# Attention scores from split queries and keys in three passes, with queries turned by one product and a transfer that exchanges halves

## The chip, the cores and the metric

The kernel runs on one core of a Trainium2 chip. A core has a TensorE (PE, the matmul array; PEld is its weight load), a VectorE (DVE), a ScalarE (ACT), a GpSimd (POOL) and a SyncE (SP), which here only issues DMA transfers. Each engine works off its own instructions in program order; semaphores tie the engines together. SBUF is the on-chip memory, PSUM the memory that the PE writes. The metric is the device time of one execution in microseconds; lower is better. The median of three runs before the change is 781.5 us (781.18 to 782.31).

## The reference

One transformer layer in fp32: cross-attention with 32 query heads and 8 key/value heads of 128, then a gated feed-forward part whose weights go through a 16-level block quantization. There are 8 batches of 128 rows, 512 wide.

```python
x = x + attention(layernorm(x), ctx, ctx, mask, Wq, Wk, Wv, Wo)
x = x + ffn(layernorm(x), w1, w2, w3)

# attention
q = apply_rope((query @ Wq).reshape(b, t, h, d))
k = apply_rope((key @ Wk).reshape(b, t, kv_h, d))
v = (value @ Wv).reshape(b, t, kv_h, d)
logits = jnp.einsum('btkgd,bTkd->bkgtT', q, k) * ATTN_MULT
logits = 30 * jnp.tanh(logits / 30)
weights = softmax(jnp.where(mask, logits, -1e30))
attn = jnp.einsum('bkgtT,bTkd->btkgd', weights, v)
return attn.reshape(b, t, h * d) @ Wo

# apply_rope; rotate_half(x) is (-x2, x1) for the halves x1, x2 of the last axis
x * cos(phase) + rotate_half(x) * sin(phase)

# ffn; dq1 to dq3 are w1 to w3 after nf4_quant_dequant: each block of 64 is divided
# by its largest magnitude, set to the nearest of 16 levels, and multiplied back
h = silu(x @ dq1.T) * (x @ dq2.T)
return h @ dq3.T
```

## The kernel before

**Products.** A number is kept as two fp32r parts, `hi` and `lo` (`split`, L154: ACT casts to `hi`, then POOL or DVE subtracts to get `lo`). A product of split operands takes three passes, hi·lo, hi·hi and lo·hi (`product`, L165), all added up in one PSUM bank. The scores are the exception: one fp32 matmul (L719, `pl`), which the profile shows as two instructions. So are the product with the values (L732, `pv`) and the transposes (L162).

**Stages.** First come the projections of keys and values (`k_proj`, `v_proj`), whose results go to DRAM (`kr_d`, `v_d`), and the first four query heads. They are one list of tiles (L611). In the tile loop (L668) a tile's evacuation is emitted one tile later, and what follows it one more. Then comes the attention loop (L807): 64 rounds. A unit `u` is one key/value head and one half of the batches; each of its four rounds takes one batch with four query heads. Round `i` holds, in the PE's order: `q_proj` of one head for unit `u + 1` (`pq`), `project(i-3)` (`po`), `turn(i-2)` (`pt_a`), `values(i-1)` (`pv`) and `scores(i)` (`pl`). The last rounds have no `q_proj`. The feed-forward part follows (`pg`, `pu`, then `pd`).

**Turning a head.** `rope` (L453) has ACT copy the two halves of 64 partitions crosswise (L461, L462), DVE multiply by the cosine (L463), POOL multiply the exchanged copy by the signed sine (L464) and add (L465) into `qr[u]`, a fresh tile for each unit, two buffers in turn.

**Scores.** ACT takes tanh and exp (L722, L723), POOL multiplies by the mask (L725). `values` divides by the sum (`ad`), `turn` transposes and splits (`aT`), and `project` adds the result to `acc`.

**The quantizer.** Its steps are spread over the stages by `pump(n)`, which adds `n` to a credit and emits steps until it is used up. A step is a comparison on ACT (L194, `nm_w`) and one on DVE (L200, or L198 for the first, `nc_w`); there are 15 for a unit of 1024 columns, and a last product (L278 or L236). The next unit is loaded midway (`w_w`, `s_w`) and normalized on POOL (L204). Its finished tiles are split and sent to DRAM (`store`, L284, transfer at L287).

**Order.** Buffers are few (raw weights three, `wq` six, `vt` two), and a load is issued by SP in program order once its buffer is free. PSUM is eight banks: two `q` banks, which `pq` and `pt_a` share in turn, one `s` for scores, one `wo`, two for `pv`, two for the quantizer (`c`).

Of the kernel before, what the change touches and what calls it, by code (L numbers as in the profile page):

```python
# [62 lines left out]
def block_kernel(ctx: ExitStack, tc: tile.TileContext, x, ctxt, mask, wq, wk, wv, wo, w1, w2, w3, w12t, w3_t,  # L63
# [145 lines left out]
    class Down(Unit):  # L209
# [30 lines left out]
        def store(self, h):  # L240
            pool, tag, bufs = (f1, "w3t", 8) if h < 8 else (nf, "nf_t", 2) if h < 10 else (xp, "wide", 2)
            t = w3t[h] = pool.tile([P, 2, KT, P], F32R, tag=tag, name=f"w3t_{h}", bufs=bufs)
            own = t.rearrange("p i k c -> p i (k c)")[:self.p].rearrange("p i (c e) -> p i e c", e=4)
            split(own[:, 0], own[:, 1], self.part(self.w, h).rearrange("p (e c) -> p e c", e=4), Q)

    class Up(Unit):
# [20 lines left out]
        def load(self):  # L267
            self.w = self.tile("nf_w", "w")
            n = min(H - self.start, self.r)
            if n < self.r:  # L270
                Q.memset(self.w, 0.0)
            for j, part in self.parts(self.w):
                nc.sync.dma_start(part[:, :, :n],
                                  w12t[j].rearrange("k p h -> p k h")[:, :, self.start:self.start + n])
            self.s = self.scale(1)

        def finish(self):
            V.tensor_tensor(self.w, self.c, self.s, ALU.mult)  # L278
            for j, part in self.parts(self.w):
                for i in range(self.r // P):  # L280
                    fresh.append(lambda tag, h=self.start // P + i, j=j, src=part[:, :, i * P:(i + 1) * P]:
                                 self.store(h, j, src))

        def store(self, h, j, src):  # L284
            t = nf.tile([P, 2, KT, P], F32R, tag="nf_t", name=f"dqt_{h}_{j}")
            split(t[:, 0], t[:, 1], src, Q)
            nc.sync.dma_start(w12t_d[h, j], t.bitcast(F32))  # L287

    class Scales:
# [5 lines left out]
        def load(self):  # L295
            self.w = nf.tile([P, 2 * D], F32, tag="nf_t", name=f"ws_{self.h}")
            rows = slice(self.h * P, min(H, self.h * P + P))
            n = rows.stop - rows.start
            if n < P:
                Q.memset(self.w, 0.0)  # L300
# [22 lines left out]
    class Scales3:  # L323
# [8 lines left out]
        def load(self):  # L332
            self.w = nf.tile([P, 2 * D], F32, tag="nf_t", name=f"ws3_{self.u}")[:, :self.cols.stop - self.cols.start]
# [12 lines left out]
        def turn(self, tag):  # L346
# [4 lines left out]
            def later():  # L351
                art = nf.tile([self.nb, 2, P], F32, tag="nf_t", name="art3")
# [11 lines left out]
    fresh, to_store, stored = [], [], []  # L364
# [8 lines left out]

    def quantize():
        invert = None
        for i, u in enumerate(units):
            for k, b in enumerate(NEG[::-1] + POS):
                u.bound(b)
# [3 lines left out]
                for when, s in found.get(i, ()):  # L382
                    if k == when - 4:
# [6 lines left out]
                if i + 1 < len(units):  # L390
                    if k == (6 if isinstance(units[i + 1], Down) else 10):
                        units[i + 1].load()
                    if k == 13:
                        units[i + 1].normalize()
# [23 lines left out]

    def wide(name, pool=xp):
# [5 lines left out]
    with ExitStack() as c1:  # L425

        xT = [wide(f"xT_{i}") for i in range(2)]
        cosq = a1.tile([P, T], F32, name="cosq")
        sgnq = a1.tile([P, T], F32, name="sgnq")
        mt = a1.tile([P, T], F32, name="mt")  # L430
        qr = {}
# [15 lines left out]
        def columns(w, h, name):  # L447
# [3 lines left out]
            return t, lambda: split(t[:, 0], t[:, 1], raw, V if name == "wk_3" else Q)  # L451

        def rope(dst, src, cos, sgn, name, engine=None, apart=False):  # L453
# [4 lines left out]

            c = src4 if engine is V and apart else tp.tile([P, 4, T], F32, tag="t1", name=f"rc_{name}")
            s = tp.tile([P, 4, T], F32, tag="t2", name=f"rs_{name}")  # L460
            S.copy(s[:hd], src4[hd:])  # L461
            S.copy(s[hd:], src4[:hd])  # L462
            V.tensor_tensor(c, src4, every(cos), ALU.mult)  # L463
            Q.tensor_tensor(s, s, every(sgn), ALU.mult)  # L464
            return lambda: (engine or Q).tensor_tensor(dst, c, s, ALU.add)  # L465
# [5 lines left out]

        def q_proj(u, g):
            kv, half = divmod(u, 2)
            if g == 0:
                qr[u] = a1.tile([P, 4, G, T], F32, tag="qr", name=f"qr_{u}", bufs=2)
            pq = bank("q", f"pq_{u}_{g}")
            w, t = wqt[kv, g], xT[half]
            product(pq, [((w[:, 0, k], w[:, 1, k]), (t[:, 0, k], t[:, 1, k])) for k in range(KT)])
            return lambda: rope(qr[u][:, :, g, :], pq, cosq, sgnq, f"q{u}_{g}", V if u < 2 else None, u == 1)


        with ExitStack() as c3:
# [6 lines left out]
            vs = a1.tile([P, 4, 4, HD], F32, tag="qr", name="vs", bufs=2)  # L489
# [55 lines left out]
            def k_proj(kv, half):  # L545
# [11 lines left out]
                def later():  # L557
                    kr = kv1.tile([P, 512], F32, tag="kr", name=f"kr_{kv}_{half}")
                    add = rope(kr.rearrange("p (b t) -> p b t", t=T), pk, tab[:, 0], tab[:, 1], f"k{kv}_{half}",
# [8 lines left out]
            def v_proj(j, b):  # L568
# [5 lines left out]
                def later():  # L574
                    v = vs[:, b % 4]
# [7 lines left out]
            def masks():  # L583
# [12 lines left out]
                def count():  # L596
# [3 lines left out]
                    V.tensor_tensor(cosq, tab[:, 0], some, ALU.mult)  # L600
                    V.tensor_tensor(sgnq, tab[:, 1], some, ALU.mult)
# [4 lines left out]
            def normal(b):  # L606
# [8 lines left out]
                     ("v", 1, 1), ("k", 7, 1)] + [("v", 1, b) for b in range(2, B)] + [("q", 0, g) for g in range(G)]  # L615
            make = {"k": k_proj, "v": v_proj, "q": q_proj}
# [40 lines left out]
            for b in range(B):  # L657
                plan[10 + (b + 1) // 2].append(lambda b=b: ln.sums(b))
                plan[18 + 2 * b].append(lambda b=b: xn.update({b: ln.rows(b)}))
                plan[19 + 2 * b].append(lambda b=b: turned.update({b: normal(b)}))  # L660
                plan[20 + 2 * b].append(lambda b=b: turned[b]())
# [5 lines left out]
            evac, last = None, None  # L667
            for n, (what, i, j) in enumerate(tiles):  # L668
                if n == 4:

                    last()
                    last = None
                done = evac() if evac else None
# [8 lines left out]
                if 9 <= n < 19:  # L682
                    store()
                if n >= 33:
                    store("wo")
                if n >= 15 and n != 17:
                    pump(2 if n in (24, 28) else 1)
            last()
            evac()()
# [8 lines left out]
        def load_o(kv, g):  # L698
# [3 lines left out]
            todo["o", kv, g] = lambda: split(t[:, 0], t[:, 1], raw, Q if kv or g > 1 else V)  # L702

        def load_kv(kv):
            for half in range(2):
                krt[kv, half] = at.tile([P, 512], F32, tag="kr", name=f"krt_{kv}_{half}", bufs=4)
                nc.sync.dma_start(krt[kv, half], kr_d[kv, half])
# [8 lines left out]
        def scores(i):  # L716
            u, kv, b, bb = where(i)
            pl = bank("s", f"pl_{i}")
            E.matmul(pl, krt[kv, u % 2][:, bb * T:(bb + 1) * T], qr[u][:, bb].rearrange("p g t -> p (g t)"),  # L719
                     start=True, stop=True)  # L720
# [26 lines left out]

        load_kv(0)
        early.append(tp.tile([P, 512], F32, tag="xn", name="raw_wo_0"))
        for g in range(G):  # L750
            load_o(0, g)
        end_store()
# [22 lines left out]
        def gate_up(half, h, pool=None, between=None):  # L775
# [18 lines left out]
            def later():  # L794
                sg = tp.tile([P, 512], F32, tag="t1", name=f"sg_{half}_{h}")
# [3 lines left out]

        due = {1: [("o", 0, g) for g in range(G)]}  # L800
# [6 lines left out]
        for i in range(N):  # L807
            u, kv, b, bb = where(i)
            s8 = i % 8
            if kv + 1 < NKV:  # L810
                if s8 == 0:
                    load_kv(kv + 1)
                if s8 < 4:
                    load_q(kv + 1, s8)
                else:
                    load_o(kv + 1, s8 - 4)
                due.setdefault(i + (2 if i < 4 else 1), []).append(("q" if s8 < 4 else "o", kv + 1, s8 % 4))
            tiles = {0: (0, 1), 1: (2,), 2: (3,), 3: ()}.get(i, (bb,)) if u + 1 < 2 * NKV else ()
            later = [q_proj(u + 1, g) for g in tiles]
            if i != 2:  # L820
                later = [f() for f in later[:1]] + later[1:]
            if i == 0:
                later.pop(0)()
            if i == 1:
                todo[due[1].pop(0)]()
            if i > 3:
                store()
                end_store()
            pump(1.5 if 3 < i < 58 else 1 if i == 58 else 0.5 if i == 3 else 0)
# [4 lines left out]
            if 0 <= i - 2:  # L834
                turn(i - 2)
            if 59 <= i < 63:
                ln.sums(i - 59)
            if i == 1:

                later.pop(0)()  # L840
            if 0 <= i - 1:
                values(i - 1)
            if i == 1:
                todo[due[1].pop(0)]()
            scores(i)
# [138 lines left out]
```

## Time and profile before

| what | value |
|---|---|
| median of the runs | 781.5 us |
| the profiled execution, whole | 781.61 us |
| its span | 779.8 us |
| instructions | 11217 |
| granted PE clock | 1.00 |
| bytes moved by DMA | 102.44 MB, mean 131 GB/s |
| PE busy, 200 to 250 us | 50.00 of 50 us |
| DVE busy, 200 to 250 us | 41.14 us |
| ACT busy, 200 to 250 us | 41.72 us |
| POOL busy, 200 to 250 us | 39.12 us |

The span is the time from the first to the last instruction on the chip; the execution's own time has a little around it. A group's line in the profile gives line, engine, operation, what it writes and reads, how often, then its busy time, the mean duration in ns, and the idle time of its engine just before it with what ended that idle time.

### The profile page before, as it was taken

To read this page: it belongs to the slowest core of one execution; us is meant where nothing else is said; L and a number is where in the kernel's file an instruction comes from. 1 tells how busy PE (TensorE), PEld (TensorE's weight loads), DVE (VectorE), ACT (ScalarE), POOL (GpSimd) and SP (SyncE) were. 2 spreads that over 40 slices of the span, in tenths; PEclk is the share of its full clock that TensorE was granted. 3 is DMA by queue.
4 is the path that set the end of the run, shared out by engine and by line. 5 is a ranking of instruction groups with operands and counts; after the bars stand their busy time and mean duration, and the time that the engine had idled before them with its cause. 6 is when DMAs were issued, how large, how long until landed. Compare 5 with 4: busy or idle time off the path is not lost.

```text
span 779.8 us, 11217 instructions
## 1 busy us (share of the span) xinstructions
PE 774.1 (99%) x3736; PEld 627.2 (80%) x3736; DVE 624.6 (80%) x850; ACT 586.2 (75%) x830; POOL 462.3 (59%) x404
## 2 busy tenths in 40 slices
PE   9999999999999999999999999999999999999998
PEld 7787877888878787877878787888778888888887
DVE  6758876988887887888888878888778697899971
ACT  7448768988897978788787879898742686789740
POOL 2559636887878778877788787878650222332100
PEclk9999999999999999999999999999999999999999
DMA  6967743546254615536245523413150235633011
GB/s 217 307 190 213 226 148 116 177 121 176 56 172 140 195 49 160 149 92 214 64 146 160 156 71 103 139 53 127 57 215 1 67 98 160 188 114 107 1 54 55
DMA packets 74497, 102.44 MB, mean 131 GB/s; under 512 B 7848, under 2 KB 44392, under 8 KB 74440
## 3 DMA queue, kind: packets, MB, share of 16 engines
q1 hardware_dynamic: 72136, 93.34, 39.5%
q0 software_dynamic: 2304, 8.39, 3.6%
q8 instruction: 30, 0.49, 0.3%
q14 instruction: 27, 0.22, 0.1%
HBM read 79.32 MB, written 22.38 MB: 130 GB/s over the span
## 4 chain that ended last, share of the span: by engine, by line
PE 94%; DMA 2%; ACT 2%; DVE 1%; issue 1%; POOL 0%; SPq 0%; POOLq 0%; DVEq 0%; ACTq 0%
PE pq L170 23%; PE po L170 23%; PE pd L170 8%; PE pg L170 8%; PE pu L170 8%; PE pv L732 7%; PE pl L719 7%; PE pt_a L162 4%; PE pvp L170 4%; PE pk L170 1%; PE pk L541 1%; DMA s_w<-scale_d 1%; DMA scale_d<-art 1%; DMA kr_d<-kr 1%; PE pt_y L162 0%
## 5 line engine op out<-in xcount | busy, mean ns | idle before, releaser
L200 DVE SCALAR_TENSOR_TENSOR nc_w<-nm_w,nc_w 128x1024 f32<-128x1024 bf16 (+1 forms) x238 | 284.5, 1195 | 54.6 <-ACT nm_w L194 43.4
L194 ACT ACTIVATE nm_w<-w_w,bias 128x1024 bf16<-128x1024 f32 (+1 forms) x255 | 275.7, 1115 | 26.9 <-POOL w_w L204 18.3
L170 PE MATMUL pq<-xT,wq 128*128 128x512 f32 x768 | 208.7, 421 | 0.0
L170 PEld LDWEIGHTS pq<-xT,wq 128*128 128x128 f32 x768 | 143.7, 188 | 56.1 <-issue 23.3
L170 PE MATMUL po<-wo,aT 128*128 128x512 f32 x768 | 188.8, 395 | 0.0
L170 PEld LDWEIGHTS po<-wo,aT 128*128 128x128 f32 x768 | 143.2, 188 | 33.4 <-issue 2.4
L725 POOL TENSOR_TENSOR th<-th,mt 128x512 f32<-128x512 f32 x64 | 83.7, 1308 | 86.3 <-ACT th L723 76.3
L464 POOL TENSOR_TENSOR rs_q<-rs_q,sgnq 128x512 f32<-128x512 f32 x64 | 82.6, 1290 | 13.6 <-ACT rs_q L462 13.4
L722 ACT ACTIVATE th<-pl 128x512 f32<-128x512 f32 x64 | 38.3, 598 | 50.9 <-PE pl L719 49.6
L465 POOL TENSOR_TENSOR qr<-rc_q,rs_q 128x512 f32<-128x512 f32 x56 | 72.6, 1297 | 0.0
L732 PE MATMUL pv<-vt,th 128*128 128x129 f32 x512 | 67.8, 275 | 0.0
L719 PE MATMUL pl<-qr,krt 128*128 128x512 f32 x128 | 65.6, 594 | 0.0
L170 PE MATMUL pg<-xT,w 128*128 128x512 f32 x264 | 63.7, 390 | 0.0
L170 PE MATMUL pu<-xT,w 128*128 128x512 f32 x264 | 63.5, 389 | 0.0
L732 PEld LDWEIGHTS pv<-vt,th 128*128 128x128 f32 x512 | 62.2, 192 | 0.4 <-POOL th L725 0.4
L170 PE MATMUL pd<-w3t,hs 128*128 128x512 f32 (+3 forms) x297 | 60.6, 366 | 0.0
L204 POOL TENSOR_TENSOR w_w<-w_w,s_w 128x1024 f32<-128x1024 f32 (+1 forms) x17 | 40.0, 2352 | 34.2 <-DMA s_w<-scale_d 32.0
L170 PEld LDWEIGHTS pd<-w3t,hs 128*128 128x128 f32 (+1 forms) x297 | 51.4, 189 | 9.2
L170 PEld LDWEIGHTS pu<-xT,w 128*128 128x128 f32 x264 | 49.5, 188 | 10.3
L170 PEld LDWEIGHTS pg<-xT,w 128*128 128x128 f32 x264 | 49.3, 188 | 10.1
L156 POOL TENSOR_TENSOR w3t<-w_w,w3t 128x512 fp32r<-128x512 f32 (+1 forms) x11 | 17.2, 1566 | 65.5 <-ACT w3t L155 65.5
L155 ACT CAST aT<-pt_a 128x512 fp32r<-128x512 f32 x64 | 36.6, 571 | 25.2 <-PE pt_a L162 25.2
(119 smaller groups left out, 1097.3 us busy)
## 6 DMA issues: line engine op xcount, KB each, us to landing
w12t_d<-dqt SPq DMA_DIRECT2D x22, 512.0 KB
s_w<-scale_d SPq DMA_DIRECT2D x40, 256.0 KB
raw_wq<-in_L_xattn_Wq SPq DMA_DIRECT2D x32, 256.0 KB
raw_wo<-in_L_xattn_Wo SPq DMA_DIRECT2D x32, 256.0 KB
w<-w12t_d POOLq DMA_DIRECT2D x16, 512.0 KB, 4.5
s_w<-scale_d SPq DMA_DIRECT2D x86, 64.0 KB
ws<-in_L_ffn_w SPq DMA_DIRECT2D x20, 256.0 KB
w_w<-in_w12t SPq DMA_DIRECT2D x10, 512.0 KB
```

The costliest lines, as they stand in the source:

```text
L155: S.copy(hi, src)
L162: E.transpose(pt[:, k * P:(k + 1) * P], src[:, k * P:(k + 1) * P], ident)
L170: E.matmul(out, a, b, start=start and i + j == 0, stop=stop and i == n - 1 and j == 2)
L194: S.activation(m, self.w, AF.Relu, bias=bias[:self.p, i:i + 1], scale=BIG if up else -BIG)
L200: V.scalar_tensor_tensor(self.c, m, step, self.c, ALU.min, ALU.subtract if i == POS[0] else ALU.add)
L204: Q.tensor_tensor(self.w, self.w, self.s, ALU.mult)
L464: Q.tensor_tensor(s, s, every(sgn), ALU.mult)
L465: return lambda: (engine or Q).tensor_tensor(dst, c, s, ALU.add)
L719: E.matmul(pl, krt[kv, u % 2][:, bb * T:(bb + 1) * T], qr[u][:, bb].rearrange("p g t -> p (g t)"), start=True, stop=True)
L722: S.activation(th, pl, AF.Tanh, scale=ATTN_MULT / CAP)
L725: Q.tensor_tensor(em[i], em[i], mt.unsqueeze(1).to_broadcast([P, G, T]), ALU.mult)
L732: E.matmul(pv[:, g, :HD + 1], em[i][:, g], vt[kv][:, b], start=True, stop=True)
```

## The change

Scores become a `product` of split keys and split queries. A key tile is loaded raw and split like a weight. The queries `hi` and `lo` live in two tiles for the whole loop: for even `u` a batch's scores read `t[:, bb]`, for odd `u` `t[:, :, bb]`, and head `g` of the next unit is written where batch `g` of this unit was read.

A head is turned by one DVE product of 1024 columns (the head times cosine, and times signed sine) out of PSUM. Two transfers then exchange the partition halves of the second part, POOL subtracts, and the result is split into the two tiles.

```diff
+        def rope_swapped(src, table, name):
+            hd = HD // 2
+            cs = halves(name)
+            V.tensor_tensor(cs, src.rearrange("p (b t) -> p b t", t=T).unsqueeze(1).to_broadcast([P, 2, 4, T]),
+                            table.unsqueeze(2).to_broadcast([P, 2, 4, T]), ALU.mult)
+            full = tp.tile([P, 4, T], F32, tag="xn", name=f"full_{name}")
+            nc.sync.dma_start(full[:hd], cs[hd:, 1])
+            nc.sync.dma_start(full[hd:], cs[:hd, 1])
+
+            def add():
+                Q.tensor_tensor(full, cs[:, 0], full, ALU.subtract)
+                return full
+            return add
...
+        def of_head(u, g):
+            if not qr:
+                qr.extend(a1.tile([P, 4, 4, T], F32R, tag="qr", name=f"qr_{j}", bufs=2) for j in range(2))
+            return [t[:, g] if u % 2 else t[:, :, g] for t in qr]
+
+        def of_batch(u, bb):
+            return [t[:, :, bb] if u % 2 else t[:, bb] for t in qr]
...
-            return lambda: rope(qr[u][:, :, g, :], pq, cosq, sgnq, f"q{u}_{g}", V if u < 2 else None, u == 1)
+            return lambda: rope_swapped(pq, cq, f"q{u}_{g}")
...
+        def load_key(kv, half):
+            raw = stage(kr_d[kv, half], [P, 512], f"kr_{kv}_{half}")
+            t = krt[kv, half] = at.tile([P, 2, 512], F32R, tag="kr", name=f"krt_{kv}_{half}", bufs=2)
+            todo["k", kv, half] = lambda: split(t[:, 0], t[:, 1], raw, Q if kv else V)
...
-            E.matmul(pl, krt[kv, u % 2][:, bb * T:(bb + 1) * T], qr[u][:, bb].rearrange("p g t -> p (g t)"),
-                     start=True, stop=True)
+            k = krt[kv, u % 2][:, :, bb * T:(bb + 1) * T]
+            product(pl.rearrange("p (g t) -> p g t", t=T), [((k[:, 0], k[:, 1]), of_batch(u, bb))])
```

Around it the order of the work moves. A finished weight tile's transfer to DRAM is put off (`leaving`) until `leave()` is called, which is before the next tile is taken from the same buffers and at the end of each round. A unit's normalization waits in `norms` until after the round's scores.

```diff
         def store(self, h, j, src):
+            leave()
             t = nf.tile([P, 2, KT, P], F32R, tag="nf_t", name=f"dqt_{h}_{j}")
             split(t[:, 0], t[:, 1], src, Q)
-            nc.sync.dma_start(w12t_d[h, j], t.bitcast(F32))
+            leaving.append(lambda: nc.sync.dma_start(w12t_d[h, j], t.bitcast(F32)))
...
-                        units[i + 1].normalize()
+                        norms.append(units[i + 1].normalize)
```

The last two value tiles come after the first four query heads, and the loop's head is rearranged:

```diff
-                     ("v", 1, 1), ("k", 7, 1)] + [("v", 1, b) for b in range(2, B)] + [("q", 0, g) for g in range(G)]
+                     ("v", 1, 1), ("k", 7, 1)] + [("v", 1, b) for b in range(2, 6)] + [("q", 0, g) for g in range(G)]
+            tiles += [("v", 1, 6), ("v", 1, 7)]
...
             if kv + 1 < NKV:
-                if s8 == 0:
+                if s8 == 2:
                     load_kv(kv + 1)
...
+            if s8 == 4 and kv + 1 < NKV:
+                load_key(kv + 1, 0)
+                due.setdefault(i + 1, []).append(("k", kv + 1, 0))
...
+            if whole and i > 3:
+                *own, full = whole.pop(0)
+                split(*of_head(*own), full, Q)
             if i > 3:
                 store()
                 end_store()
-            pump(1.5 if 3 < i < 58 else 1 if i == 58 else 0.5 if i == 3 else 0)
+            pump(2.3 if i == 4 else 2.15 if 4 < i < 58 else 2 if i == 58 else 0)
...
+            if adds and i not in (1, 2):
+                whole.append((u + 1, bb, adds.pop(0)()))
             scores(i)
...
-            pump(1.65 if 3 < i < 58 else 2 if i == 58 else 2.65 if i == 3 else 0)
+            pump(1 if 3 < i < 59 else 0)
...
+            if whole and i > 3 and bb == 3:
+                *own, full = whole.pop(0)
+                split(*of_head(*own), full, Q)
+            normalize()
+            leave()
...
+            if 0 < i < 4:
+                pump((1, 2, 0)[i - 1])
```

So in a round the head's product comes right after `pq`, the subtract before the scores, and the split in the next round, or at the end of the same round for a unit's fourth head. The memsets of the last, partly empty weight tiles (L271, L300) cover only the empty part.

## The prediction

> **What bounds the kernel now.** The page's first part comes first: busy time by engine. TensorE works for 774.1 of 779.8 us, VectorE (DVE) and ScalarE (ACT) for about 80% and 75%.
>
> ```profile
> PE 774.1 (99%) x3736; PEld 627.2 (80%) x3736; DVE 624.6 (80%) x850; ACT 586.2 (75%) x830; POOL 462.3 (59%) x404
> ```
>
> A busy PE need not be a limiting one, since matmul ends are modelled. So I read the chain of waits in order of time over the attention loop (start us, length us, what). One round of the loop, from one `pl` to the next:
>
> ```profile
> 98.42 5.50 PE pq L170 x24
> ...
> 146.07 0.86 PE pl L719 x2
> 146.93 2.76 PE pq L170 x12
> 149.70 2.74 PE po L170 x12
> 152.43 0.44 PE pt_a L162 x4
> 152.87 0.90 PE pv L732 x8
> 153.76 0.86 PE pl L719 x2
> ```
>
> The pieces touch: 146.07 to 153.76 is 7.69 us and their sum is 7.70. In this stage nothing but the PE's own rate ends any wait, so a microsecond taken off the PE is a microsecond, as long as no other engine then needs more than the shorter round. How near they are is in the groups for 165 to 550 us (385 us, 50 rounds; busy us, mean ns | idle us before, releaser):
>
> ```profile
> L200 DVE SCALAR_TENSOR_TENSOR nc_w<-nm_w,nc_w 128x1024 f32<-128x1024 bf16 x128 | 157.2, 1228 | 41.2 <-ACT nm_w L194 36.7
> L735 DVE TENSOR_TENSOR ad<-pv,rs 128x512 f32<-128x512 f32 x50 | 34.6, 691 | 1.7
> L463 DVE TENSOR_TENSOR rc_q<-pq,cosq 128x512 f32<-128x512 f32 x50 | 34.3, 686 | 13.2 <-ACT rs_q L462 13.0
> L198 DVE TENSOR_SCALAR nc_w<-nm_w 128x1024 f32<-128x1024 bf16 x9 | 11.1, 1228 | 6.9 <-ACT nm_w L194 6.7
> L278 DVE TENSOR_TENSOR w_w<-nc_w,s_w 128x1024 f32<-128x1024 f32 x9 | 10.9, 1215 | 0.0
> L177 DVE RECIPROCAL ar<-ar 128x16 f32<-128x16 f32 x11 | 2.7, 245 | 0.2 <-POOL ar L176 0.2
> ...
> L725 POOL TENSOR_TENSOR th<-th,mt 128x512 f32<-128x512 f32 x50 | 65.2, 1305 | 68.2 <-ACT th L723 59.9 <-DVE aT L156 5.8 <-DMA s_w<-scale_d 1.8
> L465 POOL TENSOR_TENSOR qr<-rc_q,rs_q 128x512 f32<-128x512 f32 x50 | 64.9, 1297 | 0.0
> L464 POOL TENSOR_TENSOR rs_q<-rs_q,sgnq 128x512 f32<-128x512 f32 x50 | 64.3, 1285 | 0.0
> ...
> L461 ACT COPY rs_q<-pq 64x512 f32<-64x512 f32 x50 | 29.2, 584 | 4.2 <-PE pq L170 3.1
> L462 ACT COPY rs_q<-pq 64x512 f32<-64x512 f32 x50 | 28.9, 579 | 0.6
> ```
>
> DVE's idle times add up to 41.2+1.7+13.2+6.9+0.2 = 63.2 us, 1.26 a round. I count idle rather than busy, because back-to-back instructions overlap by about 0.08 us in the timeline and durations overstate the load. Summed in the same way over all their groups, ACT idles 58.1 us (1.16 a round) and POOL 83.4 (1.67).
>
> **PE.** The fp32 `pl` costs 0.86 us a batch. Its replacement is three fp32r passes of 128x512, the form of `pq`: 5.50/24 = 0.229 each, 0.69 for three. So 0.17 saved a score, times 64 = **11.0 us**. Bounds: the stretches x12 give 2.74 to 2.77, so 0.69 at most and 10.7 to 11.2 in all. One thing no row shows: for odd `u` the moving operand is four runs of 128 columns, 2 KB apart, where every row has one run. If that brought those 32 scores back to 0.86, only half, 5.5 us, would be left; I take no cost, since the matmul sees the same 512 columns.
>
> The Trainium skill ("TensorE: Matmul & The Clock Gate", section "Wait — 56ns, not 53.3ns?") has 215.7 ns from start to start of a warm 512-column matmul; the trace has 229, at a granted clock of 1.00. By the page the three passes would take 0.65 and the saving would be 13.6 us; the trace decides.
>
> **DVE.** Per head the 512-wide `rc_q` product (0.686) becomes one of 1024 columns from PSUM (L278 has that form: 1.215), +0.53 a round; two of the old ones would be 1.37, so +0.69 at most. I take 0.53, the same shape. The quantizer's credits stay 3.15 a round (1.5+1.65 before, 2.15+1 after). Round 7.52: idle falls to 1.26-0.17-0.53 = **0.56**. That is 7%, but the 0.26 of waiting for `rs_q` goes too, because the product needs nothing from ACT any more.
>
> **ACT.** Two half copies (0.584+0.579) go; one cast of the turned head comes (the 128x512 casts of `wq` take 0.605) and 16 key casts over 64 rounds, 0.15. Balance -0.4: idle 1.16-0.17+0.4 = 1.39.
>
> **POOL.** Multiply and add (1.285+1.297) become subtract and split subtract (`wq` splits: 1.292): no change. Key splits add 16x1.3/64 = 0.33. Idle 1.67-0.17-0.33 = 1.17. `normalize()` moves behind the round's mask: the same 2.39 us (L204) a unit, and ACT's first comparison with its result comes some three quantizer steps later, about a round; without that, ACT and then DVE's next step wait up to 2.4 us a unit, 26 in all. The memsets of L271 and L300, now of the empty part alone, save 1.9 us once, off the path.
>
> **The exchanged halves.** This is new: 64 heads, two transfers of 128 KB each, 16.8 MB over some 450 us, beside 131 GB/s on average: 37 GB/s more. What counts is latency, since POOL's subtract waits for it and the mask multiply of the same round stands behind it. Let `pq` end at 0. The product ends at 1.3. Two issues on SP take 0.7 (L287 at 0.33 each in the timeline) to 1.3 (L263 at 0.63). No row shows an on-chip copy; the nearest chain entries are these:
>
> ```profile
> 17.70 3.23 DMA raw_wv<-in_L_xattn_Wv
> 23.04 4.05 DMA kr_d<-kr
> 43.62 1.99 DMA scale_d<-art
> 46.38 5.82 DMA s_w<-scale_d
> ```
>
> So halves land between 1.3+0.7+2.0 = 4.0 and 1.3+1.3+5.8 = 8.4; I take 5.2, from the plain 256 KB load. Then subtract to 6.5, mask to 7.8, and for the fourth head the split to 9.1. Deadlines, by the pieces of the round: the masked scores are read by `pv` at 7.52+3.18 = 10.7, the fourth head by `pl` at 11.6. Both hold by over 2 us, and landing may slip to 8.1 (10.7 less two POOL operations) or 7.7 (11.6 less three). SP is in order, so a swap also stands behind whatever was issued before it. The kernel before lets stores wait on SP for unfinished splits (up to 12.6 us, 120 in all, at L287); `leave()` puts such a store off to the end of the round, and its split is ahead of that round's subtract and mask on POOL. The raw loads that wait for buffers come after the round's swap in the program and are released by splits of earlier rounds. This is why I cost SP at nothing; without that cover, a store waiting 12 us would hold the swap past 8.1.
>
> The skill speaks against this step: "DMA: Bandwidth & Descriptors", section "Rules for kernel authors", says two transfers to disjoint partition halves only serialize, and one of 128 partitions is better. No run here shows it. By its fit (section "Anatomy of one DMA", measured on another queue), 2.0 us plus bytes over 436 GB/s, I estimate 2.6 us for both.
>
> **The start.** Rounds 0 to 3 fill the pipeline. Before, the chain there shows `pv` 1.12 instead of 0.89, and `pq` 3.01 and 2.85 instead of 2.75: 0.6 us of stalls. After, four first heads must be turned, swapped and split. The last has two value tiles and two `pq` of cover (4x2.75 = 11.0 us) for 1.2+0.7+3.2+1.3+0.6+0.7 = 7.7 (10.9 with the slow ends). But those rounds now also hold three quantizer steps (before: 3.15 in round 3) and splits on DVE. Bounds -0.6 to +3; I take +0.7.
>
> **Sum.** The profiled execution took 781.61 us, span 779.8 plus 1.8 around it; the median of the runs is 781.5, so no correction. 781.6 - 11.0 + 0.7 = **771.3 us**, with 769.5 to 774.5 for this case alone (saving 10.7 to 11.2, other bounds -0.6 to +3, rounded outward).
>
> **Rivals.** *A, the swap comes late.* Rounds that load a quantizer unit put 512 KB of weights plus scales before the next swap; about 11 such rounds lie in the loop (54x3.15/16). At the slow end, 8.4, the mask is 0.3 late and a fourth head 0.7: with 0.7 for each, 7.7 more, **779.0**. For it: s_w's 5.82 us. Against: SP is free to issue these loads right after a swap, so they have most of a round to drain. Decides from a landing at 8.1.
>
> *B, slower: DVE becomes the bound.* Its load without idle is 7.69-1.26+0.53 = 6.96. If its waits for ACT's comparisons stay (36.7+6.7 over 50 rounds, 0.87) and the 0.04 others, a round takes 7.87, 0.18 longer than before. Some 58 rounds: +10.4; the six last rounds, without queries, still save 1.0: **791.0**. For it: 62 of 137 comparisons are waited for, in order. Against: these are waits of an engine with time to spare, on an ACT that itself waits for `pl` and `pt_a` and gets lighter. Decides once more than 0.56 us of idle a round remains.
>
> *C, strided passes cost as much as fp32:* 771.3+5.5 = **776.8**. Only the missing row speaks for it.
>
> **How the numbers follow.** Forecast 0.68, A 0.12, B 0.14, C 0.04, a dearer start 0.02. A measurement of this kernel can't tell less than 0.2%, 1.6 us, from no change. Faster: 0.68, C's 0.04 and some 0.07 of A's spread round 779, together 0.79; slower: B, and 0.02 of A; the remaining 0.05 is no change. The range 769.3 to 780 takes in forecast, C and most of A and leaves B out.
>
> **What would show it.** Right: the loop's rounds at 7.52 in the chain, `pl` x3 at 0.69, DVE idle near 0.5 a round, the exchange waited for by POOL alone and under 1.5 us a round. Wrong: `pl` of odd units longer than of even ones (C); PE idle ended by POOL's mask or split with the swap behind it (A); PE idle ended by DVE's `aT`, `ad` or the 1024-column product (B).

## The result and the profile after

| kernel | median, us | ratio to before, 95% interval | first `pl` | loop | behind it |
|---|---|---|---|---|---|
| before | 781.3 | | 115.5 | 476.1 | 188.2 |
| after | 815.5 (810.8 to 818.4) | 1.0433 [1.0395, 1.0471] | 119.2 | 501.1 | 196.3 |
| e1, no exchange | 783.5 | 1.0032 [1.0015, 1.0048] | 119.9 | 467.8 | 198.3 |
| e2, one load of a unit | 808.3 | 1.0348 [1.0318, 1.0378] | 119.0 | 496.9 | 192.0 |
| e3, loads on ACT's ring | 808.4 | 1.0344 [1.032, 1.0367] | 121.9 | 489.0 | 197.1 |
| e4, halves by ACT copies | 792.2 | 1.014 [1.0115, 1.0166] | 119.0 | 476.3 | 197.0 |
| e5, e4 and one load | 786.3 | 1.0064 [1.0039, 1.0089] | 116.8 | 476.6 | 190.9 |
| e6, e1 and one load | 779.5 | 0.9977 [0.996, 0.9995] | 119.9 | 468.3 | 191.6 |
| e7, swap first, loads behind it | 815.8 | 1.0435 [1.0387, 1.0482] | 120.6 | 501.0 | 192.4 |
| e8, e7 and more value tiles | 810.0 | 1.0378 [1.0325, 1.043] | 115.2 | 502.6 | 190.7 |
| e9, e8, loads two steps earlier | 797.2 | 1.0199 [1.0182, 1.0216] | | | |
| e10, e9, units one step earlier | 815.2 | 1.0452 [1.0423, 1.0481] | 116.1 | 504.8 | 192.0 |
| e11, e5 and more value tiles | 785.0 | 1.0044 [1.0031, 1.0058] | 114.6 | 475.6 | 192.9 |
| e12, copies only behind loads | 782.4 | 1.0012 [0.9997, 1.0026] | 114.1 | 473.9 | 192.8 |

Each ratio is against runs of before made beside that kernel. The loop is counted from the first `pl` to the first `pg` of each profiled execution, and what is behind it ends with the span. The profiled execution of e9 was 12 us longer than its three others (796.1 to 797.2) and is left out, its stages with it.

The change made the kernel slower by 4.3%, 34 us, where 10 us less were forecast. In the profiled execution (818.40 us, span 816.6) 3.7 us are lost ahead of the loop, 25.0 in it and 8.1 behind it. The forecast for the loop was 11 us less, so 36 us have to be found there.

First the page's busy times and the chain by engine:

```profile
PE 779.4 (95%) x3800; PEld 645.5 (79%) x3800; DVE 656.6 (80%) x851; ACT 551.8 (68%) x782; POOL 479.8 (59%) x419
...
PE 47%; DMA 14%; POOL 10%; issue 9%; ACT 8%; DVE 7%; SPq 4%; POOLq 0%; DVEq 0%; ACTq 0%
```

The PE's share of the chain fell from 94% to 47%, while DMA holds 14% and POOL 10%. The PE is busier than before by 5 us, though its work became lighter. The changed kernel's chain over one whole round and a late one shows how (start us, length us, what):

```profile
269.51 0.69 PE pl L170 x3
270.20 2.77 PE pq L170 x12
272.97 2.74 PE po L170 x12
275.70 0.44 PE pt_a L162 x4
276.14 0.89 PE pv L793 x8
277.03 0.69 PE pl L170 x3
...
285.25 2.78 PE pq L170 x12
...
288.76 1.23 DVE cs_q L490
...
290.06 0.49 SPq L493
...
290.91 6.99 DMA full_q<-cs_q
...
298.03 0.06 POOL full_q L497
...
299.25 1.28 POOL th L786
...
300.58 1.16 PE pv L793 x8
```

The round 269.51 to 277.03 is the one forecast: 7.52 us, with `pl` at 0.69. The swap of the round that begins at 285.25, issued at 290.06, lands at 297.89, 9.86 us after the end of `pq` (288.03). The deadline worked out in advance was 8.1; so the mask should be 1.8 us late. Counting 10.7 from the end of `pq`, `pv` was due at 298.7 and starts at 300.58: 1.85 late. What SP issued beside this swap (start, length, queue and line, what):

```profile
283.02 0.47 SPq L493 DMA_DIRECT2D full_q<-cs_q  x1
283.54 0.59 SPq L494 DMA_DIRECT2D full_q<-cs_q  x1
284.22 0.54 SPq L460 DMA_DIRECT2D raw_wo<-in_L_xattn_Wo  x1
284.81 0.92 SPq L305 DMA_DIRECT2D ws<-in_L_ffn_w  x2
285.77 0.43 SPq L274 DMA_DIRECT2D w_w<-in_w12t  x1
286.25 1.29 SPq L264 DMA_DIRECT2D s_w<-scale_d  x2
287.58 0.61 SPq L338 DMA_DIRECT2D ws<-in_L_ffn_w  x1
290.06 0.49 SPq L493 DMA_DIRECT2D full_q<-cs_q  x1
290.91 0.50 SPq L494 DMA_DIRECT2D full_q<-cs_q  x1
```

The trace lists these loads with 256 KB a raw tile, 256 a `ws` of L305 and an `s_w` of L264, and the other two have 512: 256+512+512+512+512 = 2304 KB between two swaps, right behind the first of them. The stretches of this time (length, busy time of PE, PEld, DVE, ACT and POOL, granted clock, DMA share, GB/s) show the 16 DMA engines full when the second swap arrives:

```profile
284.00:290.00 6.00, 6.00 (x31) 5.00 (x30) 5.68 (x8) 4.97 (x8) 3.96 (x4) 1.00 0.92 275
290.00:294.00 4.00, 4.00 (x25) 3.45 (x24) 3.73 (x6) 1.93 (x5) 2.60 (x3) 1.00 1.10 221
```

Over the whole kernel, the groups (busy us, mean ns | idle us before, releaser):

```profile
L497 POOL TENSOR_TENSOR full_q<-cs_q,full_q 128x512 f32<-128x512 f32 x64 | 83.8, 1309 | 106.6 <-DMA full_q<-cs_q 80.8 <-DVE acc L807 9.6 <-ACT th L784 7.5
...
L490 DVE TENSOR_TENSOR cs_q<-pq,cq 128x1024 f32<-128x1024 f32 x64 | 77.7, 1214 | 2.4 <-PE pq L170 1.4 <-POOL full_q L497 0.9
...
L793 PE MATMUL pv<-vt,th 128*128 128x129 f32 x512 | 70.0, 280 | 18.2 <-POOL th L786 18.0
...
L170 PE MATMUL pl<-qr,krt 128*128 128x512 f32 x192 | 62.2, 433 | 5.4 <-POOL qr L156 3.1 <-ACT art L322 2.2
```

Of the 64 swaps, POOL waited for 32, 80.8 us in all. From SP's first issue to POOL's subtract these took 4.04 us in the mean, but 20 of them 2.9 to 3.3 us, and six 5.8 to 9.0, each with a burst of loads before it.

The PE's waits for POOL come to 18.0+3.1 = 21 us. The rest of the loop's loss is not waiting. The three stretches of the loop in which the granted clock was 0.50, and the PE's timeline around the first:

```profile
210.87:217.70 6.83, 6.18 (x15) 4.83 (x16) 4.42 (x6) 4.33 (x7) 5.99 (x6) 0.50 0.16 41
436.15:442.98 6.83, 5.73 (x18) 4.86 (x19) 4.72 (x7) 4.25 (x7) 6.67 (x6) 0.50 0.02 8
528.31:531.73 3.42, 3.42 (x10) 2.65 (x10) 1.01 (x1) 2.16 (x4) 3.42 (x3) 0.50 0.12 36
```

```profile
207.99 1.16 PE L793 MATMUL pv<-vt,th 128*128 128x129 f32 x8
211.52 1.65 PE L170 MATMUL pl<-qr,krt 128*128 128x512 f32 x3 [2.37 <-POOL qr L156]
212.97 5.11 PE L170 MATMUL pq<-xT,wq 128*128 128x512 f32 x12
```

Within an idle time of 2.37 us (209.15 to 211.52) the granted clock falls to 0.50 and stays there for 6.83 us, and a `pq` of 2.77 us takes 5.11. Not every such wait does this: behind one of the same 2.37 us, which ended at 386.79, the clock stayed at 1.00 (384 to 392 us). In the three stretches the PE works for 6.18+5.73+3.42 = 15.3 us, which at 1.00 would be about 7.7; so the clock costs the loop some 7.7 us, an estimate from these rows. The Trainium skill ("TensorE: Matmul & The Clock Gate", section "What's actually happening") has a clock of 4/8 after an idle window of some 3.4 us; the half rate agrees, while the idle time seen here was shorter than that window.

Behind the loop, SP loads one unit of the quantizer twice (timeline of the changed kernel):

```profile
694.27 0.83 SPq L232 DMA_DIRECT2D w_w<-in_w3t  x2
695.14 4.63 SPq L226 DMA_DIRECT2D s_w<-scale_d  x8
701.07 1.05 SPq L232 DMA_DIRECT2D w_w<-in_w3t  x2
703.48 7.91 SPq L226 DMA_DIRECT2D s_w<-scale_d  x16
```

The new condition at L404 asks for `len(ups)`, meaning the list of the units of `w1` and `w2`. But L823 binds the name `ups` anew, to an empty list to which `gate_up` appends one entry a call. In the loop its length is 0; behind it, it grows, and for one unit the test is true at step 6 and again at step 9.

### The profile page after: what moved, and what is told of

The parts are those of the page before. It is cut to its first block, busy times and chain, and to the rows that moved or that the text cites. A ratio compares the mean times of both kernels' runs of the same rounds, so it can differ in the third digit from the quotient of the medians.

```text
span 816.6 us, 11543 instructions
## 1 busy us (share of the span) xinstructions
PE 779.4 (95%) x3800; PEld 645.5 (79%) x3800; DVE 656.6 (80%) x851; ACT 551.8 (68%) x782; POOL 479.8 (59%) x419
## 3 DMA queue, kind: packets, MB, share of 16 engines
q0 software_dynamic: 2304, 8.39, 3.2%
## 4 chain that ended last, share of the span: by engine, by line
PE 47%; DMA 14%; POOL 10%; issue 9%; ACT 8%; DVE 7%; SPq 4%; POOLq 0%; DVEq 0%; ACTq 0%
PE po L170 12%; PE pq L170 12%; DMA full_q<-cs_q 7%; PE pv L793 5%; ACT nm_w L194 4%; PE pl L170 4%; PE pd L170 3%; DVE nc_w L200 3%; POOL th L786 3%; PE pk L582 2%; DMA w_w<-in_w3t 2%; PE pg L170 2%; DMA v_d<-v 2%; PE pt_a L162 2%; PE pu L170 2%
## 5 line engine op out<-in xcount | busy, mean ns | idle before, releaser
L170 PE MATMUL pq<-xT,wq 128*128 128x512 f32 x768 | 191.7, 400 | 0.0
L170 PEld LDWEIGHTS pq<-xT,wq 128*128 128x128 f32 x768 | 147.5, 192 | 34.5
L497 POOL TENSOR_TENSOR full_q<-cs_q,full_q 128x512 f32<-128x512 f32 x64 | 83.8, 1309 | 106.6 <-DMA full_q<-cs_q 80.8
L793 PE MATMUL pv<-vt,th 128*128 128x129 f32 x512 | 70.0, 280 | 18.2 <-POOL th L786 18.0
L490 DVE TENSOR_TENSOR cs_q<-pq,cq 128x1024 f32<-128x1024 f32 x64 | 77.7, 1214 | 2.4 <-PE pq L170 1.4
L155 ACT CAST qr<-full_q 128x512 fp32r<-128x512 f32 x63 | 38.9, 618 | 57.6 <-POOL full_q L497 57.6
L156 POOL TENSOR_TENSOR qr<-full_q,qr 128x512 fp32r<-128x512 f32 x58 | 75.3, 1298 | 0.4
L170 PE MATMUL pg<-xT,w 128*128 128x512 f32 x264 | 65.6, 398 | 3.4 <-ACT sg L856 3.4
L170 PE MATMUL pl<-qr,krt 128*128 128x512 f32 x192 | 62.2, 433 | 5.4 <-POOL qr L156 3.1
```

The source lines that it names most:

```text
L155: S.copy(hi, src)
L156: engine.tensor_tensor(lo, src, hi, ALU.subtract)
L170: E.matmul(out, a, b, start=start and i + j == 0, stop=stop and i == n - 1 and j == 2)
L490: V.tensor_tensor(cs, src.rearrange("p (b t) -> p b t", t=T).unsqueeze(1).to_broadcast([P, 2, 4, T]), table.unsqueeze(2).to_broadcast([P, ...
L497: Q.tensor_tensor(full, cs[:, 0], full, ALU.subtract)
L793: E.matmul(pv[:, g, :HD + 1], em[i][:, g], vt[kv][:, b], start=True, stop=True)
```

## The experiments

The theory after the first look: the exchange, late behind bursts of loads, costs the loop its 36 us (by waits and the clock); the double load costs most of the 8 behind it; two value buffers cost the start.

**e1, no exchange.**

```diff
-            nc.sync.dma_start(full[:hd], cs[hd:, 1])
-            nc.sync.dma_start(full[hd:], cs[:hd, 1])
...
-                Q.tensor_tensor(full, cs[:, 0], full, ALU.subtract)
+                Q.tensor_tensor(full, cs[:, 0], cs[:, 1], ALU.subtract)
```

> The exchange of the halves is left out: POOL subtracts the second product straight from the first, so the scores are of unexchanged halves, and no transfer stands between DVE and POOL. Work on every engine stays the same but for SP and the DMA rings. Theory (the exchange lands late): the attention loop, 501 us from the first pl to the first pg, loses its stalls, 36 us against the 465 expected from 64 shorter scores; 777 to 784 us in all, POOL no longer idle before its subtract by more than 0.3 us a round. Rival (DVE or POOL have too much work for the shorter round): 805 us or more, and the PE still waits for POOL's mask.

Measured: 783.5 us, so the exchange costs 32.0; the loop takes 467.8, 33.3 less than in the changed kernel and 2.7 above the forecast of 465.1 (476.1-11.0). The three passes, the wide DVE product and the added splits are all still there, so none of these is the cause. e6 is the same with one load of the unit, and its loop stands beside that of the changed kernel here, the line of the changed kernel first:

```profile
119.20:620.30 501.10, 478.59 (x2438) 398.21 (x2439) 424.11 (x535) 358.53 (x513) 378.03 (x329) 0.98 0.54 154
```

```profile
119.90:588.20 468.30, 466.98 (x2439) 392.28 (x2438) 424.63 (x534) 358.89 (x513) 378.85 (x329) 1.00 0.43 130
```

The PE's instructions are the same, 2438 and 2439. The 32.8 us between the two are 21.2 of PE idle time (501.10-478.59 against 468.30-466.98) and 11.6 of PE busy time. Of these 11.6, some 7.7 go with the granted clock, as worked out above. Another 3 can be put down to `pv`, which takes 1.16 us where it waited for POOL (300.58 in the chain) and 0.89 where it did not, 11 times in the loop; this too is an estimate.

**e2, one load of the unit.**

```diff
-                    if k == (9 if i in (len(ups) - 1, len(ups)) else 6 if isinstance(units[i + 1], Down) else 10):
+                    if k == (6 if isinstance(units[i + 1], Down) else 10):
```

> Only the point at which a down unit is loaded is fixed at its seventh step; in the changed kernel the order of instructions shows the unit of rows 768 loaded twice, at its predecessor's seventh and tenth step. Theory (the second load costs the feed-forward part its extra 8 us): about 808.5 us (806 to 811), and the feed-forward part from the first pg to the end back at 188 to 190 us from 196. Rival (the feed-forward part is late because the loop leaves a backlog of weights): unchanged, 813 to 818 us.

Measured: 808.3, 7.2 less, with 192.0 us behind the loop instead of 196.3 (188 to 190 were expected). SP's timeline of e2 at the same place:

```profile
690.39 0.83 SPq L232 DMA_DIRECT2D w_w<-in_w3t  x2
691.26 14.42 SPq L226 DMA_DIRECT2D s_w<-scale_d  x16
```

The unit is loaded once, and 3.4 us for which `pg` waited for ACT in the changed kernel are gone. The profiled loop was 4.2 us shorter too, which the one load can't have done, since both loads lie behind the loop; runs of these kernels spread by several microseconds (after: 810.8 to 818.4). So 4.3 is the better figure for the double load.

**e3, the loads on another ring.** Only the engine that issues the quantizer's loads changes (L264, L274, L305, L338):

```diff
-                nc.sync.dma_start(part[:, :, :n],
+                nc.scalar.dma_start(part[:, :, :n],
```

> The quantizer's loads of weights and scales for the up units and of rows for the scales are issued by ACT and so stand in ACT's ring; the exchange stays on SP. ACT has some 0.7 us more of issuing a round. Theory (the exchange stands behind these loads in one ring): a landing of 3 us instead of up to 8, most stalls gone, 783 to 797 us. Rival (the copy is slow by itself, or the 16 engines are short of bandwidth): the wait of POOL's subtract for the transfer stays near 80 us in all, 808 us or more.

Measured: 808.4, 7.1 less than the changed kernel, with the loop at 489.0. The expectation is missed: the swaps that POOL waited for took 4.20 us in the mean (4.04 in the changed kernel), again six of them 5.1 to 9.0. One of the six, from three timelines of e3:

```profile
190.36 0.82 ACTq L305 DMA_DIRECT2D ws<-in_L_ffn_w  x2
...
192.60 0.63 ACTq L264 DMA_DIRECT2D s_w<-scale_d  x1
...
195.28 0.47 SPq L493 DMA_DIRECT2D full_q<-cs_q  x1
...
201.79 1.29 POOL L497 TENSOR_TENSOR full_q<-cs_q,full_q 128x512 f32<-128x512 f32 x1 [5.22 <-DMA full_q<-cs_q]
```

This swap took 6.51 us. ACT had issued 1536 KB on its own ring from 190.36 to 193.23, while SP had issued one raw tile (256 KB, at 188.70) and 16 KB since the swap before. So a burst under way delays the swap from the other ring too; the order within one ring is not the whole cause. No run separates the number of bytes from the kind of load: all six long swaps of the changed kernel had `w_w` and `s_w` ahead of them. The Trainium skill ("DMA: Bandwidth & Descriptors", section "Queues, rings and completion order") has each of the DMA engines go round robin over the rings for which it has work, a packet at a time; by that a swap on a ring of its own should take turns with the burst and not stand behind the whole of it. The landings here don't show it. The loop was 12 us shorter than in the changed kernel all the same, with 12.1 us of PE waits for POOL instead of 21.1; why is not shown.

**e4, the halves by ACT.**

```diff
             def add():
+                full = tp.tile([P, 4, T], F32, tag="xn", name=f"full_{name}")
+                S.copy(full[:hd], cs[hd:, 1])
+                S.copy(full[hd:], cs[:hd, 1])
                 Q.tensor_tensor(full, cs[:, 0], full, ALU.subtract)
```

> The exchange is made by two copies of 64 partitions on ACT, right before POOL's subtract, in place of the two transfers. Theory (only the transfer's latency is at fault): about 1.2 us of ACT a round, of 1.39 us reckoned idle; 778 to 790 us. Rival (ACT then is full and becomes the bound, or the shorter round is too short for the other engines): 800 us or more, with DVE and PE waiting for ACT.

Measured: 792.2, 2 us past the upper end. The loop takes 476.3, as long as before the change. The PE waits no longer for POOL's mask; POOL now waits 58.4 us for ACT's copies in the loop, which cost ACT 2 x 0.62 us a head, and the loop is 8.5 us longer than e1's.

**e6 and e5, the savings together.** e1 and e4, each with e2's condition.

> Leaves out: the exchange of halves (as in e1), and the second load of unit w3 rows 768 (as in e2); the queries are turned wrongly. If the late exchange and the double load are two separate costs, both savings add: 783.5 (e1) - 7.2 (e2: 815.5 to 808.3) = 776.3 us, and the feed-forward part is back at some 190 us with no load of that unit's rows issued twice. If the double load only cost what the late exchange had left over (one shared cause), the time stays near 783. What is then left of 776 against the forecast of 771.3 is the start (first pl at about 119 instead of 116).

> e4 (792.2 us: the halves are exchanged by two ACT copies at the subtract, not by DMA) without the second load of unit w3 rows 768. If the double load's cost adds here too: 792.2 - 7.2 = 785.0 us (783 to 787). If the feed-forward part had been hidden behind something else in e4: 789 to 792.

Measured: 779.5 and 786.3. The double load is worth 4.0 us beside e1 and 5.8 beside e4, not 7.2, which goes with the 4.3 above. e6 was expected at 776.3; so even with no exchange and one load the change gains 0.2% (0.9977). Its profile (781.6, with a span of 779.8) misses the forecast of 771.3 by 10.3: 3.7 at the start (119.9 against 115.5+0.7), 3.2 in the loop, 3.4 behind it.

**e7, the swap first.** The quantizer's loads are kept in a list in rounds 4 to 57, and SP issues them directly behind the next round's swap; the condition is e2's.

```diff
+                after_swap(lambda j=j, part=part: nc.sync.dma_start(
+                    part[:, :, :n], w12t[j].rearrange("k p h -> p k h")[:, :, self.start:self.start + n]))
...
+            load_held()
+            hold[:] = [1] if 3 < i < 58 else []
             if kv + 1 < NKV:
                 if s8 == 2:
```

> The exchange stays as it is, on SP; the loads of quantizer units, of their scales and of the rows for new scales, which after issues wherever the quantizer is, are held back in rounds 4 to 57 and issued by SP directly behind the next round's swap (with the second load of unit w3 rows 768 gone too, as in e2, 808.3 us). Same bytes, same ring, same engines; only the order changes. Theory (a swap lands late because 1.4 to 2.2 MB were issued in the 6.5 us before it): nearly all swaps land in 2.9 to 4 us, the subtract's wait for the exchange falls from some 80 us to under 25, the loop takes 468 to 478 us and the whole 776 to 786. Rival (a copy on the chip is slow by itself, or the average traffic slows it, whatever was issued before): the landings stay at 6 to 9 us in the same rounds and the time at 800 to 810. A second rival: the held loads come so late that DVE and POOL wait for them; then those waits show at L200 and L204 and the time is between.

Measured: 815.8, 7.5 more than e2 (776 to 786 were expected). The swaps land as the theory has it, and the time doesn't follow: of 34 swaps that POOL waited for, 28 took up to 3.3 us and none 5, with a mean of 3.16. But now the loads come late. POOL's timeline of e7 at its worst place (idle time before in brackets):

```profile
474.79 1.28 POOL L156 TENSOR_TENSOR qr<-full_q,qr 128x512 fp32r<-128x512 f32 x1
481.75 2.35 POOL L204 TENSOR_TENSOR w_w<-w_w,s_w 128x1024 f32<-128x1024 f32 x1 [5.68 <-DMA s_w<-scale_d]
484.06 1.26 POOL L508 TENSOR_TENSOR full_q<-cs_q,full_q 128x512 f32<-128x512 f32 x1
485.29 1.27 POOL L797 TENSOR_TENSOR th<-th,mt 128x512 f32<-128x512 f32 x1
```

POOL stands at the normalization, waiting for scales that were issued behind the swap. The subtract of a swap that was issued at 473.7 begins at 484.06, and the mask follows it. DVE's waits for `ws` rise in the same way, from 0.5 us in e2 to 22.5. In the loop the PE waits 12.0 us for DVE's `acc` (1.1 in the changed kernel) and 7.8 for POOL (21.1). The burst and the swap want the same engines in the same few microseconds, and in-order POOL and DVE pay whichever comes second.

**e8, more value tiles.** e7, with the value tiles up to (1, 3) in the two query buffers, eight deep.

```diff
+            vs = [a1.tile([P, 4, 4, HD], F32, tag="qr", name=f"vs_{i}", bufs=2) for i in range(2)]
...
-                    pool, tag, bufs = (wp, "wq", 6) if (j, b) in ((1, 6), (1, 7)) else (kv1, "vs", 2)
-                    v = pool.tile([P, 4, HD], F32, tag=tag, name=f"v_{j}_{b}", bufs=bufs)
+                    if j and b > 3:
+                        pool, tag, bufs = (wp, "wq", 6) if b > 5 else (kv1, "vs", 2)
+                        v = pool.tile([P, 4, HD], F32, tag=tag, name=f"v_{j}_{b}", bufs=bufs)
+                    else:
+                        v = vs[b // 4][:, b % 4]
```

> e7, and the value tiles lie in the two query buffers again (eight deep, up to the tile (1, 3); the rest as in after). Theory: the start's extra 3.7 us come from ACT waiting for value tiles of two buffers only (10.7 us at L619): that wait goes, the first pl comes at 115 to 117 us instead of 119 and the whole is 2 to 3.5 us under e7. Rival: the start is longer because of the turned first heads themselves (product, swap, split, three quantizer steps in rounds 0 to 3): then the first pl still comes at 118 to 119.5 and e8 equals e7.

Measured: 810.0, 5.8 less (2 to 3.5 were expected), and the first `pl` at 115.2. That is 5.4 earlier than in e7 and slightly earlier than before the change. The waits of all engines show what went; this is the changed kernel, and in e8 the line is gone:

```profile
ACT v L619 <- DMA v_d<-v: 10.7, 4, 5.6
```

**e9 and e10, the held loads asked for earlier.**

```diff
-                    if k == when - 3:
+                    if k == when - (3 if i < 1 else 5):
...
-                    if k == (6 if isinstance(units[i + 1], Down) else 10):
+                    if k == (5 if isinstance(units[i + 1], Down) else 8):
```

e10 has 4 and 7 in place of 5 and 8.

> e8 (swap first, loads behind it; 810.0 us), with the held loads asked for two quantizer steps earlier (rows for new scales 5 steps ahead of their use instead of 3, units at step 8 instead of 10, and at 5 instead of 6). In e7 and e8 the swaps landed in 3 us and the time stayed: theory now is that the same burst of bytes, put behind the swap, came too late itself (DVE waits 24.6 us for the rows ws at L175, POOL 17.6 for s_w at L204, and the subtract stands behind POOL's wait). Then with two steps more these two waits fall to under 15 us together, the swaps still land in 3 to 3.5 us, the loop takes 475 to 490 us instead of 502.6 and the whole 782 to 797. Rival: the landing of the swap was never the matter, and the bytes (37 GB/s more of them) slow every transfer: the time stays at 805 to 812. Third possibility: the earlier loads wait for a buffer with the swap behind them on SP; then SP's waits at the load lines rise and swaps land late again.

> e9 with the units asked for one step earlier still (7 and 4 instead of 8 and 5). If POOL's wait for s_w at L204 is what is left, 1 to 5 us under e9; if a buffer is waited for now, as much above it.

Measured: 797.2 and 815.2. Two steps earlier gain 12.8 us, just outside what was expected; one more step for the units loses 18. In e10 DVE waits 0.5 us for `ws`, but the swaps are late again, with a mean of 3.94 and seven over 5 us. Over the loop, e10's POOL waits this long (total, times, longest):

```profile
POOL full_q L508 <- DMA full_q<-cs_q: 92.4, 32, 9.6
```

In e10 the rows for new scales (12-5) and the units are both asked for at step 7, so they fall behind the same swap: five of the seven long swaps follow one behind which SP issued 1536 KB of them (L305, L274, L264). Whether this is what turns 797 into 815 is not shown, since the trace of e9 is of its long execution. No place that was tried for the loads brought the time back to that of before.

**e11 and e12, in search of a faster version.** e11 is e5 with e8's value tiles.

> e5 (786.3 us: halves exchanged by two ACT copies, one load of w3 rows 768) with the value tiles in the two query buffers as in e8. In e8 the first pl came 5.4 us earlier than in e7. e5's first pl is at 116.8, so less is to be had here: 1 to 4 us, 782 to 785, which would be no faster than before (781.0).

Measured: 785.0, 1.3 less than e5. e12 takes e11 and chooses for each head as it is emitted:

```diff
+            quiet = not recent
+            if not start:
+                recent.clear()
+            if quiet:
+                there = tp.tile([P, 4, T], F32, tag="xn", name=f"full_{name}")
+                nc.sync.dma_start(there[:hd], cs[hd:, 1])
+                nc.sync.dma_start(there[hd:], cs[:hd, 1])
 
             def add():
-                full = tp.tile([P, 4, T], F32, tag="xn", name=f"full_{name}")
-                S.copy(full[:hd], cs[hd:, 1])
-                S.copy(full[hd:], cs[:hd, 1])
+                full = there if quiet else tp.tile([P, 4, T], F32, tag="xn", name=f"full_{name}")
+                if not quiet:
+                    S.copy(full[:hd], cs[hd:, 1])
+                    S.copy(full[hd:], cs[:hd, 1])
```

> e11 (785.0 us), but a head's halves go by the two transfers of the change where no quantizer load was issued since the swap before it (40 of 64 heads, all behind round 3), and by the two ACT copies elsewhere (24 heads). Theory: a swap lands in 3 us unless a burst of loads stands before it, and it is ACT's two copies (1.24 us a round) that hold e11's loop at 475.6 us against 468 without an exchange. Then the subtract waits for DMA no longer than 4 us in any round, ACT has 40 x 1.24 = 50 us less to do, and the loop takes 468 to 473 us: 777.5 to 782.5 in all, about the time of before (781.5), perhaps the first version under it. Rival (the transfers' bytes slow the other loads or land late anyway, even in these rounds): the subtract's waits for DMA come to over 5 us in several rounds and the time is 787 to 800.

Measured: 782.4, with 1.0012 [0.9997, 1.0026] no different from before. The loop takes 473.9, 0.9 past the expected end. POOL's waits from 119 to 590 us, for the 40 heads that go by DMA and the 24 that go by ACT:

```profile
POOL full_q L509 <- DMA full_q<-cs_q: 24.7, 19, 3.5
...
POOL full_q L509 <- ACT full_q L508: 17.2, 12, 2.5
```

Where no load of the quantizer was issued since the last swap, the exchange comes in time. Of the versions that compute the whole layer and use the three passes, this is the fastest, and it is not under the kernel before.

## Why the prediction was wrong

**The bound and the sum for the PE: right.** The PE's rounds are 7.52 us where nothing is late, `pl` takes 0.69 for odd and even units alike (rival C falls), and without the exchange the loop comes to 467.8 where 465.1 was forecast.

**DVE, ACT, POOL: right.** The product of 1024 columns takes 1.214 us (1.215 forecast). Fifty rounds of e6, without the exchange:

```profile
165.00:541.00 376.00, 376.00 (x1955) 316.77 (x1953) 342.72 (x419) 301.18 (x426) 317.76 (x262) 1.00 0.44 131
```

The PE works all of the time, in rounds of 7.52 us. DVE idles 0.67 us a round ((376.00-342.72)/50; 0.56 forecast), ACT 1.50 (1.39) and POOL 1.16 (1.17). DVE does not become the bound, so rival B falls.

**The exchanged halves: the step that failed.** "So halves land between 1.3+0.7+2.0 = 4.0 and 1.3+1.3+5.8 = 8.4; I take 5.2, from the plain 256 KB load." In a quiet round the total was right, partly by luck, since two errors cancel: the product ended 2.0 after `pq` and not 1.3 (288.03 to 289.99 in the round shown, 2.07 in the median of the 64 heads), and from there the swap took some 3.0 and not 3.9. Behind a burst the landing was 9.86, past the upper end of the bounds. That end was one transfer's duration from a row of before and had no term for the bytes of other transfers still under way. What the runs showed in its place: with these loads issued behind the swap (e7) no swap that POOL waited for took over 4.2 us, and with them ahead of it (the changed kernel) up to 9.0. The burst could be seen beforehand. Rival A counted "512 KB of weights plus scales before the next swap"; SP's timeline of before already has 512 KB each of `ws`, `w_w` and `s_w` within 2.6 us, and a raw tile behind them:

```profile
404.73 0.33 SPq L334 DMA_DIRECT2D ws<-in_L_ffn_w  x1
405.15 0.89 SPq L273 DMA_DIRECT2D w_w<-in_w12t  x1
406.10 1.25 SPq L263 DMA_DIRECT2D s_w<-scale_d  x2
```

In the round shown two more loads of `ws` (L305) came with them. That made 2304 KB (2.4 MB) from 284.22 on, and until the second swap landed the DMA engines moved 231 GB/s in all. "Most of a round to drain" is 7.5 us, or 1.7 MB at that rate. What has not landed yet counts, not what was issued: 1792 KB were issued between the swaps of 323.09 and 330.49, but the engines moved 332 and 345 GB/s from 326 to 328 and from 328 to 330 us, and the swap of 330.49 took 2.98.

**The deadlines: right.** A landing at 8.1 decides; 9.86 made `pv` 1.85 late, as the arithmetic has it.

**SP costed at nothing: right as it was meant.** The deferred store waits little at its line (9.6 us in the loop, 2.3 at most); what held the swaps was not an instruction ahead of them on SP. e3 shows it: taking these loads off SP's ring didn't shorten the landings.

**Rival A: the right mechanism, at a quarter of its price.** It had 11 rounds at 0.7 us, 7.7 in all. The PE waited for POOL 13 times, 21.1 us in all, 1.6 each; to this come 11.6 us more of busy time, some 7.7 of them by the lower granted clock, which no part of the prediction had, since the clock of before was 1.00 throughout the loop. Together, 32.8 instead of 7.7. The sign that the exchange would be waited for under 1.5 us a round could not tell the two apart: POOL's 80.8 us are 1.26 a round, but the six late swaps hold 33 of them.

**The start: +0.7 forecast, +3.7 measured**, past the upper bound of +3. The turned first heads cost nothing that e8 shows (115.2 against 115.5 before), though e8 has eight places for the value tiles where the kernel before had four. The value tiles' move from four places to two stands in the diff and was not costed.

**Behind the loop: not in the prediction.** 8.1 us, of which 4.3 go with the double load (e2). The other 3.4 to 3.8 remain in e2 and e6; in e6, 2.2 us of it are PE idle time in the last 60 us (5.5 from 720 us to the end, against 3.3 before). Its cause stays open.

## What to carry to other kernels

A small transfer on the path of every round has to be costed with the bytes that may be under way when it is issued, summed over all loads between two of its issues, and not with the duration of a lone one; a separate ring did not protect it here. A stall of the PE costs more than its length where the clock falls behind it. And a condition that uses a name bound again further down, or a tile that gets fewer buffers, is a step of the change like any other.

## What was not expected of the hardware

- A swap of 256 KB within SBUF took 2.9 to 3.3 us from its first issue in quiet rounds and 5.8 to 9.0 behind a burst, also with the burst on another ring (e3: 5.1 to 9.0).
- Within a PE idle time of 2.37 us the granted clock fell to 0.50, for 6.83 us; another idle time of the same length left it at 1.00. In the changed kernel's loop three such stretches, 17.1 us in all, cost some 7.7 us.
